# Four-block cross-attention decoder on one core: self attention steps of the last block set among cross steps, queries, keys and values in one arena, the last feed forward in three groups

## The chip, the cores and the metric

The kernel runs on one core of one Trainium2 chip. The metric is the device time of one launch in microseconds (us). All data are float32. In the profile PE is the matmul engine (TensorE), PEld its weight loads, DVE the vector engine, ACT the scalar engine, POOL GpSimd, SP the queue that issues most DMAs. `mm` and `s` are PSUM tiles, all else in these lines is SBUF.

## The reference

Input `x` is 8 batches of 112 rows of 256; the context `ctx_768` is 8 batches of 375 rows of 192. Four blocks follow each other, each adding to `x`:

```
block 0, 1:  x += SelfAttention(norm(x))       16 heads of 64
             x += CrossAttention(norm(x), ctx) 16 heads of 64, 375 keys
             h = norm(x) @ Wp + bp;  a, gate = halves of h (1024 each)
             x += (a * gelu(gate)) @ Wf + bf
block 2:     x += CrossAttention(norm(x), ctx) 16 heads of 64
block 3:     x += SelfAttention(norm(x))       16 heads of 16, causal and key mask
             x += CrossAttention(norm(x), ctx) 16 heads of 16, key mask
             x += gelu(norm(x) @ mlp1 + b1) @ mlp2 + b2        (1024 inner)
```

Attention is softmax(q k^T scaled) v per head, then an output product and its bias. `norm` is a layer norm with gain and bias. The blocks' weights differ.

## The kernel before

**Stages.** The ten lines above are stages 0 to 9: 0 self, 1 cross, 2 feed forward, 3 self, 4 cross, 5 feed forward, 6 cross (block 2), 7 self, 8 cross and 9 feed forward (block 3). `x` lies in seven tiles of 128 rows, the 896 rows of all batches one after another, so a tile spans two batches, and `last_batch(t)` is the last batch that tile `t` needs. `hT` (normed input, transposed) and `oT` (attention output or the feed forward's inner values, transposed, 8 pieces of 128) are one tensor each, for all 896 columns, written and read in parts by all stages.

**Steps.** Attention is cut into steps in the list `steps`: 2 a batch in stages 0 and 3 (8 heads each), 4 a batch in stages 1, 4, 6 and 8 (4 heads each), 1 a batch in stage 7 (16 heads). A step (`add_step`) has three parts on PE: S, the scores into a tile of `ps_s` (L905); T, transposes of the probabilities in banks of four (L924), evicted to `wT`; and PV (L948), evicted to `oT`. Between S and T lies the softmax. In stages 1, 4 and 6 it is a negated maximum on DVE (L872), exponentials on ACT with their sums (L878), a reciprocal on DVE (L884) and a multiplication of each probability tile on POOL (L885). In stages 7 and 8 DVE adds the mask and finds the bound in one instruction a head (L861), ACT takes the exponentials (L865), and the division comes after PV: item R takes reciprocals (L982) and POOL copies them to `rb` (L983); item N transposes `rb` on PE (L989), evicts it as `rT`, and POOL scales `oT` with it (L993).

**Items.** Everything else is an `Item` of a planner (`Plan`), with a cost, a due step (`deadline`), what it uses, what it makes and what it depends on. `add_products` multiplies `oT` by an output weight for one row tile (L587), adds it to `x` (L591), and runs the next stage's norm: statistics on DVE (L525, L527, L529), a power on POOL (L531), the normed tile `xn` on POOL (L533), the bias row added to `x` on POOL (L535). `add_norm_transposes` makes a group of `hT` (L556); the groups are tiles 0-1, 2-3, 4-5 and 6. `add_pair_projection` makes four q or k units for a pair of batches (L620); `add_last_projection` and `add_self_values` do the same for block 3 (L642, L669). Keys and values of the context are jobs in two halves (L710 and L719 for keys, L744 and L753 for values; in stage 8 also L787 to L809), of which up to two are opened at the end of a step and closed at the start of the next one. The function `evac` chooses ACT or DVE for an eviction by a running estimate of their load.

**Order.** PE's instructions run in the order in which the planner emits them; the other engines' are ordered by the framework's scheduler. The list of steps falls into three segments: stages 0 and 1, 3 and 4, 6 to 8. A feed forward's items belong to the next segment. In each iteration the planner emits S of step i+2, PV of step i, T of step i+1, and between the T banks fillers that are ready, earliest due first, as many as `pace` asks for:

```python
for i in range(lo - 2, hi):
    left = plan.pace(i, seg)
    plan.close_jobs()
    plan.main(("S", i + 2)); plan.main(("PV", i))      # where these exist
    for k in range(n):
        plan.main(("T", i + 1, k))
        left -= plan.fill(min(left, share))
    plan.fill(left)
    plan.open_jobs(2, i + 3.5)
```

What is not there when a step needs it is emitted just before it (`require`). Ahead of a segment `drain` emits whatever is ready until the first steps' inputs exist, and after the last step until nothing is left. Items that make q, k or v aren't taken over 8 steps ahead of their due step.

**Buffers.** Weights pass through a ring of 7 buffers, bias rows through one of 2; loads are issued on SP in the order of the `add_*` calls as buffers come free. The ring also holds the mask bytes (`m8`) and two buffers `cm` of masks for four batches each, which come right after `m8` in that order. `add_masks` makes the self mask `cmask` (L495, L496) and eight context masks (L514), all on POOL. q, k and v have rings of 8, 9 and 9 buffers (448, up to 448, and 512 elements a partition). PSUM has four `mm` tiles and two `s` tiles.

**Last feed forward.** `ff_stage` (L1159 matmuls, L1166 GELU on ACT straight from PSUM) takes columns in two groups, `FFG = [(0, 512), (512, 384)]`, after the last step's S; `add_products` then takes the seven row tiles and writes them out.

## Time and profile before

| | us |
|---|---|
| median of 3 runs | 1685.27 (1681.66 to 1685.77) |
| the profiled execution | 1682.51 |
| its span, first to last instruction | 1680.7 |
| granted clock, mean | 0.998 |

| stage | first S at, us | | stage | first S at, us |
|---|---|---|---|---|
| 0 self | 29.5 | | 6 cross | 1094.4 |
| 1 cross | 170.9 | | 7 self | 1398.0 |
| 3 self | 558.6 | | 8 cross | 1460.5 |
| 4 cross | 696.4 | | 8, last S | 1618.9 |

The three feed forwards' matmuls stand at 468.9 to 525, 1005 to 1071 and 1625 to 1667. An engine's busy time is the union of its instructions' times. Matmuls are pipelined and their ends are modelled, so short gaps between them count as busy. In a line of the timeline the columns are the start, the length, the engine, the line of the code, the operation, output<-inputs, shape and count, and in brackets the idle time of the engine before it with what ended it. In a line of waits they are who waited for whom, us in total, times, the longest. In a line of stretches they are the stretch, its length, busy time and count of PE, PEld, DVE, ACT and POOL, the clock granted to PE, the DMAs' share and GB/s.

### The profile page before, as it was taken

To read this page: it belongs to the slowest core of one execution; us is meant where nothing else is said; L and a number is where in the kernel's file an instruction comes from. 1 tells how busy PE (TensorE), PEld (TensorE's weight loads), DVE (VectorE), ACT (ScalarE), POOL (GpSimd) and SP (SyncE) were. 2 spreads that over 40 slices of the span, in tenths; PEclk is the share of its full clock that TensorE was granted. 3 is DMA by queue.
4 is the path that set the end of the run, shared out by engine and by line. 5 is a ranking of instruction groups with operands and counts; after the bars stand their busy time and mean duration, and the time that the engine had idled before them with its cause. 6 is when DMAs were issued, how large, how long until landed. Compare 5 with 4: busy or idle time off the path is not lost.

```text
span 1680.7 us, 30104 instructions
## 1 busy us (share of the span) xinstructions
PE 1644.6 (98%) x11740; PEld 1139.4 (68%) x11740; DVE 847.6 (50%) x2275; ACT 750.0 (45%) x2390; POOL 730.6 (43%) x705
## 2 busy tenths in 40 slices
PE   8999999999999999999999999999999999899999
PEld 7777666666657878676666665766666667666657
DVE  3454454555532344445545552245554558877751
ACT  3454444444431444344444442144443447766661
POOL 1323455556632223355655660474546654332210
PEclk9999999999999999999999999999999999999999
DMA  5011020000101011000000010000000010000000
GB/s 185 4 50 56 3 86 1 1 26 1 51 29 44 1 29 51 26 1 29 2 1 26 1 45 29 11 26 1 1 20 1 1 40 30 2 2 2 2 1 22
DMA packets 26564, 39.48 MB, mean 23 GB/s; under 512 B 1543, under 2 KB 21559, under 8 KB 26423
## 3 DMA queue, kind: packets, MB, share of 16 engines
q1 hardware_dynamic: 25495, 36.74, 6.9%
q8 instruction: 92, 1.51, 0.4%
q10 hardware_dynamic: 864, 0.79, 0.1%
q14 instruction: 49, 0.40, 0.1%
q0 software_dynamic: 64, 0.05, 0.0%
HBM read 35.88 MB, written 0.92 MB: 22 GB/s over the span
## 4 chain that ended last, share of the span: by engine, by line
PE 87%; DVE 5%; issue 3%; ACT 3%; POOL 2%; DMA 0%; POOLq 0%; ACTq 0%; DVEq 0%
PE mm L587 11%; PE mm L620 11%; PE s L905 10%; PE mm L924 10%; PE mm L948 9%; PE mm L710 8%; PE mm L744 7%; PE mm L1159 5%; PE mm L719 4%; PE mm L753 4%; PE mm L669 4%; DVE pr L861 2%; ACT pr L865 2%; PE mm L642 1%; PE mm L556 1%
## 5 line engine op out<-in xcount | busy, mean ns | idle before, releaser
L885 POOL TENSOR_SCALAR pr<-pr,rinv 112x375 f32<-112x375 f32 x384 | 468.8, 1239 | 347.0 <-DVE rinv L884 346.9
L878 ACT ACTIVATE pr<-s,nm 112x375 f32<-112x375 f32 (+1 forms) x640 | 301.8, 489 | 169.6 <-DVE nm L872 169.6
L924 PE MATMUL mm<-ident,pr 112*128 112x112 f32 (+2 forms) x1920 | 233.6, 264 | 10.2 <-ACT oT L307 3.7
L924 PEld LDWEIGHTS mm<-ident,pr 112*128 112x128 f32 (+2 forms) x1920 | 208.6, 151 | 45.9 <-issue 14.0
L872 DVE TENSOR_REDUCE nm<-s 112x2 f32<-112x750 f32 (+1 forms) x224 | 206.4, 958 | 59.3 <-PE s L905 55.3
L307 ACT COPY wT<-mm 128x448 f32<-128x448 f32 (+2 forms) x271 | 141.8, 531 | 180.1 <-PE mm L924 180.0
L948 PEld LDWEIGHTS mm<-wT,v 128*64 128x64 f32 (+5 forms) x3840 | 159.6, 129 | 81.7 <-issue 34.1
L905 PE MATMUL s<-kT,qT 64*112 64x375 f32 (+3 forms) x1792 | 207.2, 392 | 0.0
L948 PE MATMUL mm<-wT,v 128*64 128x112 f32 (+5 forms) x3840 | 200.6, 264 | 3.0 <-ACT wT L307 1.9
L905 PEld LDWEIGHTS s<-kT,qT 64*112 64x112 f32 (+1 forms) x1792 | 112.8, 173 | 73.4 <-issue 22.9
L889 POOL TENSOR_TENSOR pr<-pr,rinv 112x896 f32<-112x896 f32 x32 | 53.9, 1684 | 214.4 <-DVE rinv L888 196.0
L865 ACT ACTIVATE pr<-pr,nm 112x112 f32<-112x112 f32 (+1 forms) x256 | 123.9, 486 | 50.9 <-DVE nm L861 50.8
L315 DVE COPY wT<-mm 128x448 f32<-128x448 f32 (+2 forms) x209 | 125.8, 612 | 16.6 <-PE mm L924 14.1
L878 ACT ACTIVATION_READ_ACCUMULATOR pr<-s,nm 112x1 f32 x640 | 133.1, 208 | 0.0
L315 DVE COPY kT<-mm 128x375 f32<-128x375 f32 (+1 forms) x117 | 65.4, 559 | 131.4 <-PE mm L719 115.5
L315 DVE COPY v<-mm 128x512 f32<-128x512 f32 (+2 forms) x73 | 50.5, 692 | 139.3 <-PE mm L753 119.0
L307 ACT COPY kT<-mm 128x375 f32<-128x375 f32 (+1 forms) x107 | 51.2, 478 | 130.9 <-PE mm L719 118.3
L531 POOL TENSOR_TENSOR rs<-ve,mhalf 128x1 f32<-128x1 f32 x70 | 39.5, 565 | 144.5 <-DVE ve L529 141.9
L591 DVE TENSOR_TENSOR x<-mm,x 128x256 f32<-128x256 f32 x70 | 29.5, 421 | 132.5 <-PE mm L587 132.5
L884 DVE RECIPROCAL rinv<-sums 112x1 f32<-112x1 f32 x384 | 62.6, 163 | 66.8 <-ACT pr L878 57.4
L710 PE MATMUL mm<-ctxA,L_xattn_Wk 128*128 128x375 f32 x256 | 91.5, 480 | 0.4 <-ACT hT L303 0.4
L744 PE MATMUL mm<-L_xattn_Wv,ctxA 128*128 128x512 f32 (+1 forms) x192 | 90.8, 595 | 0.4 <-ACT hT L303 0.4
(140 smaller groups left out, 2364.7 us busy)
## 6 DMA issues: line engine op xcount, KB each, us to landing
L_xattn_Wo<-in_L_xattn_Wo_dram SPq DMA_DIRECT2D x3, 1024.0 KB, 17.8
L_xattn_w_ff<-in_L_xattn_w_ff_dram SPq DMA_DIRECT2D x3, 1024.0 KB, 5.2
L_xattn_Wv<-in_L_xattn_Wv_dram SPq DMA_DIRECT2D x4, 512.0 KB, 6.2
L_xattn_Wq<-in_L_xattn_Wq_dram SPq DMA_DIRECT2D x2, 1024.0 KB, 4.9
L_xattn_Wp<-in_L_xattn_Wp_dram SPq DMA_DIRECT2D x2, 1024.0 KB, 5.3
L_xattn_wq<-in_L_xattn_wq_dram SPq DMA_DIRECT2D x2, 1024.0 KB, 4.7
L_xattn_wo<-in_L_xattn_wo_dram SPq DMA_DIRECT2D x2, 1024.0 KB, 5.3
L_xattn_mlp_w<-in_L_xattn_mlp_w_dram SPq DMA_DIRECT2D x2, 1024.0 KB, 4.9
```

Of the source, the lines that this page charges most:

```text
L307: nc.scalar.copy(dst, src)
L315: nc.vector.tensor_copy(dst, src)
L587: nc.tensor.matmul(ps[:, :D], lhsT=oT[:, c, t * P : (t + 1) * P], rhs=got[wv or w][:, c, :], start=(c == 0), stop=(c == n - 1),)
L620: nc.tensor.matmul(ps[:, i * 2 * T : (i + 1) * 2 * T], lhsT=got[w][:, k, m * P : (m + 1) * P], rhs=hT[:, k, lo:hi], start=(k == 0), stop=( ...
L710: nc.tensor.matmul(ps[:, :S], lhsT=got[wv][:, (2 * u + i) * P : (2 * u + i + 1) * P], rhs=ctxA[:, cols], start=True, stop=False,)
L744: nc.tensor.matmul(ps[: KCH[c][1], :], lhsT=lhs(ctxA, slice(0, KA), c), rhs=got[w][:, hf * 512 : (hf + 1) * 512], start=True, stop=False,)
L872: nc.vector.tensor_reduce(nm[:, :, :ns], sv, AX.X, ALU.max, negate=True)
L878: nc.scalar.activation(pr[:, bk, sl, :], sv[:, bk, sl, :], AF.Exp, bias=nm[:, bk, sl : sl + 1], accum_out=sums[:, bk, sl : sl + 1],)
L885: nc.gpsimd.tensor_scalar_mul(pr[:, bk, sl, :], pr[:, bk, sl, :], rinv[:, bk, sl : sl + 1])
L905: nc.tensor.matmul(tiles[i][:, n % 2, (n // 2) * nk : (n // 2 + 1) * nk], lhsT=qap(h), rhs=kap(h), start=True, stop=True,)
L924: nc.tensor.transpose(pt[:kl, i * T : (i + 1) * T], cell[h][:, c * P : c * P + kl], ident[:T, :T])
L948: nc.tensor.matmul(po[p0 : p0 + dp, blk * T : (blk + 1) * T], lhsT=got[vk][:kl, hv * dp : (hv + 1) * dp], rhs=wt, start=(c == 0 and par(h) ...
```

## The change

It does five things. (1) Steps: the eight self steps of stage 7 no longer stand between stages 6 and 8. Batch 0's stands after the second cross step of batch 4 of stage 6, batches 1 to 3 after the second of batches 5 to 7; batches 4 to 7 after the second step of batches 0 to 3 of stage 8. Due steps are now looked up in `at[(stage, batch, part)]`. (2) q, k and v lie in one tensor of 12224 elements a partition, the size of the three rings together; `find` takes the lowest free place for q and k and the highest for v; a place is free when every item that uses its key has been emitted. (3) The last feed forward takes its first layer in groups of 512, 256 and 128 columns, due within stage 8; the first two groups are evicted with their bias alone, and GELU runs later over `oT` in place, four pieces at a time, after the last exponentials. (4) The `cm` buffers come after the `kv` weights in the order of loads, and the masks' due steps change. (5) The look-ahead is 7 steps, and a job isn't opened ahead of its segment. Dependencies that held block 3's k and v back until stage 6 had made its last are gone. The rest of the code only moves.

```diff
+LASTG = [(0, 512), (512, 256), (768, 128)]
...
+    def find(self, keys):
+        held = sorted(p for k, p in self.place.items() if self.refs.get(k, 0) > 0)
+        out = []
+        for k in keys:
+            n, at = self.size(k), None
+            if k[0] == "v":
+                end = self.arena
+                for lo, hi in reversed(held):
+                    if end - hi >= n:
+                        break
+                    end = lo
+                at = end - n if end >= n else None
+            else:
+                at = 0
+                for lo, hi in held:
+                    if lo - at >= n:
+                        break
+                    at = hi
+                at = at if at + n <= self.arena else None
...
-            if len(self.opened) == n or it.deadline > until:
+            if len(self.opened) == n or it.deadline > until or it.seg > seg:
                 break
...
-            if it.deadline > self.step + 8 and any(k[0] in self.rings for k in it.makes):
+            if it.deadline > self.step + self.ahead and any(k[0] in "qkv" for k in it.makes):
                 continue
...
-    RINGS = {"w": 7, "q": 8, "k": 9, "v": 9, "row": 2}
+    RINGS = {"w": 7, "row": 2}
+    ARENA = 12224
...
+    arena = const.tile([P, ARENA], F32, name="arena")
...
+    def place(key):
+        lo, hi = plan.place[key]
+        t = arena[:, lo:hi]
+        return t if hi - lo != 4 * T else t.rearrange("p (i t) -> p i t", i=2)
...
-        plan.add(Item(("mask", "self"), 0, self_mask, info[7][1] - 14, uses=[src], seg=SEG[6]))
+        plan.add(Item(("mask", "self"), 0, self_mask, first_of(7, 0) - 8, uses=[src], seg=SEG[6]))
+        yield
...
-                plan.add(Item(("mask", b), 0, ctx_mask, info[7][1] + b, uses=[src, key], seg=SEG[7]))
+                plan.add(Item(("mask", b), 0, ctx_mask, first_of(8, b) - 5, uses=[src, key], seg=SEG[7]))
...
-                t = (qpool if ring == "q" else kpool).tile([P, 2, 2 * T], F32, tag=ring, name=ring + "T")
+                t = place(key)
...
-        after = [(("kj", 6, B - 1, 3), 0)] if ring == "k" else []
...
+    per = {0: 2, 1: 4, 3: 2, 4: 4, 6: 4, 7: 1, 8: 4}
+    order = [[(st, b, g) for b in range(B) for g in range(per[st])] for st in (0, 1, 3, 4, 6, 8)]
+    after = {(6, 4): 0, (6, 5): 1, (6, 6): 2, (6, 7): 3, (8, 0): 4, (8, 1): 5, (8, 2): 6, (8, 3): 7}
+    ff_at = {}
+    for i, part in enumerate(order):
+        for st, b, g in part:
+            (self_step if st in (0, 3) else cross_step)(st, 16 if st == 8 else 64, b, g)
+            if g == 1 and (st, b) in after:
+                self_step(7, 16, after[(st, b)], 0)
...
+    def last_ff(st, w1, bias):
+        for f, (lo, n) in enumerate(LASTG):
+            ready = last_of(8, last_batch(tiles_of(lo, lo + n)[-1]))
...
+                    dst = oT[:, m, lo : lo + n]
+                    if f < 2:
+                        evac(dst, ps[:, :n], n, None, col(bias, m))
+                    else:
+                        tc.keep_in_program_order(nc.scalar.activation(dst, ps[:, :n], AF.Gelu, bias=col(bias, m)))
...
+                        ("ff", st, f, m), 8 * n / 2400, fn, ready + (3.5 + 0.7 * m, 2.5 + 0.2 * m, 5 + 0.1 * m)[f],
...
+                def fn(lo=lo, n=n):
+                    for m in (0, 4):
+                        v = oT[:, m : m + 4, lo : lo + n]
+                        tc.keep_in_program_order(nc.scalar.activation(v, v, AF.Gelu))
...
+                        deps=[(("ff", st, f, m), 1.0) for m in range(8)] + [(("S", len(steps) - 1), 4.0)],
...
-    add_masks()
+    masks = add_masks()
+    next(masks)
...
     add_last_ctx(w("kv"), L3 + "k_w", L3 + "v_w")
+    next(masks, None)
     add_row(("row", 8), L3 + "out_b")
...
-            plan.open_jobs(2, i + 3.5)
+            plan.open_jobs(2, i + 3.5, seg)
```

## The prediction

> **What bounds the kernel now.** I read the page first, then the busy time by stretch, the timeline of the places where PE stands still, and the list of waits. The page's engine line and the busy line of the matmul engine in 40 slices:
>
> ```profile
> PE 1644.6 (98%) x11740; PEld 1139.4 (68%) x11740; DVE 847.6 (50%) x2275; ACT 750.0 (45%) x2390; POOL 730.6 (43%) x705
> ...
> PE   8999999999999999999999999999999999899999
> ```
>
> PE is the bound, and the change takes no matmul away. It can win only what PE loses, 1680.7 - 1644.6 = 36.1 us of idle and any half-speed time. So I asked where that lies: busy time of each engine in stage 6 (blocks' third cross attention), stage 7 (the self steps), stage 8 in two parts, and the tail.
>
> ```profile
> 1135.00:1380.00 245.00, 244.56 (x1699) 162.41 (x1699) 131.31 (x304) 105.93 (x297) 135.96 (x117) 1.00 0.03 10
> 1395.00:1460.00 65.00, 57.17 (x747) 45.38 (x745) 57.47 (x343) 51.72 (x263) 19.88 (x34) 1.00 0.06 20
> 1460.00:1560.00 100.00, 95.37 (x999) 62.47 (x998) 75.35 (x253) 66.11 (x198) 28.52 (x48) 1.00 0.01 2
> 1560.00:1623.00 63.00, 57.28 (x680) 37.39 (x676) 49.61 (x176) 45.13 (x137) 14.64 (x22) 1.00 0.01 2
> 1623.00:1680.00 57.00, 53.55 (x248) 37.02 (x248) 7.12 (x18) 14.89 (x26) 3.68 (x6) 1.00 0.05 17
> ```
>
> Columns are length, then PE, PEld, DVE, ACT, POOL busy, granted clock, DMA share, GB/s. Stage 6 loses 0.4 us in 245. Stages 7 and 8 lose 7.8, 4.6 and 5.7 us, with DVE at 88%, 75% and 79%: softmax there is short of matmuls to hide behind. One more loss is at the start of stage 6, first on POOL, then on PE, then in the clock column:
>
> ```profile
> 1116.99 4.84 POOL L514 TENSOR_SCALAR cm<-m 112x375 f32<-112x375 uint8 x4
> 1121.91 0.57 POOL L531 TENSOR_TENSOR rs<-ve,mhalf 128x1 f32<-128x1 f32 x1
> 1122.46 2.47 POOL L885 TENSOR_SCALAR pr<-pr,rinv 112x375 f32<-112x375 f32 x2
> 1124.91 2.46 POOL L533 TENSOR_SCALAR xn<-x,mv,rs 128x256 f32<-128x256 f32 x2
> ```
> ```profile
> 1121.37 0.87 PE L556 MATMUL mm<-ident,xn 128*128 128x128 f32 x6
> 1126.21 0.69 PE L556 MATMUL mm<-ident,xn 128*128 128x128 f32 x2 [3.97 <-POOL xn L533]
> ```
> ```profile
> 1125.00:1130.00 5.00, 3.79 (x16) 3.56 (x17) 1.58 (x3) 1.35 (x3) 5.00 (x6) 0.50 0.17 60
> 1130.00:1135.00 5.00, 5.00 (x18) 3.19 (x16) 0.00 (x0) 1.00 (x2) 1.19 (x1) 0.84 0.07 22
> ```
>
> Four context masks stand on POOL ahead of a norm; PE waits 3.97 us and then runs at half clock. Last, the tail on PE:
>
> ```profile
> 1627.85 1.30 PE L948 MATMUL mm<-wT,v 128*32 128x112 f32 x24
> ...
> 1629.57 12.18 PE L1159 MATMUL mm<-hT,L_xattn_mlp_w 128*128 128x512 f32 x28
> ...
> 1656.69 10.48 PE L1159 MATMUL mm<-hT,L_xattn_mlp_w 128*128 128x384 f32 x32
> 1667.01 10.52 PE L587 MATMUL mm<-L_xattn_mlp_w,oT 128*128 128x256 f32 x48
> ```
>
> After the last PV (L948) PE runs dense: two thirds of the last first-layer matmuls and all its products.
>
> **The change, part by part**, against this execution (span 1680.7, time 1682.5; the median of the runs is 1685.3, 2.8 above it).
>
> *Context masks moved.* Eight L514 of 1.16 us leave the start of stage 6 for its end: their buffers now queue behind `kv`. Without the 4.84 us, L531 starts at 1117.1 and xn is ready near 1122, when PE asks. Saved: the wait, 3.97; the clock, 3.79 x 0.50 + 5.00 x 0.16 = 2.7; together 6.7. L531 and L533 stay, so I take 6.2 (bounds 0, if something else stands in front of xn, and 6.7). The 9.3 us of masks land in POOL's idle 45% of stage 6; should that cover go, each costs at most its 1.16. The self mask (L495, L496) stays where it was, since `drain` still emits it when nothing else is ready.
> The trace has the clock at 0.50 after 3.97 us of idle. [...]
>
> *Self steps among cross steps.* Eight steps of 7.8 us each (their score matmuls start from 1398.0 to 1453.0; stage 8's first at 1460.5). Four go into batches 4 to 7 of stage 6. A step brings ACT 16 exps at a 0.37 us period, 6.0 us, and DVE 16 x 0.19 = 3.1 us, beside evictions. Stage 6 has 9.6 us of PE a step with ACT 43% and DVE 54% busy; four cross steps and one self step come to ACT about 54% and DVE 59%. Cover is ample: these four lose nothing, -3.9 (half of 7.8). The other four stand in batches 0 to 3 of stage 8. Half of stage 8 plus half of stage 7 is DVE 90, ACT 80, PE 107 us: DVE at 85%, hardly better than now, so -1.1. Sum -5.0. Bounds: -12.4 (all of 7.8 + 4.6) and +2 (the mix idles 12% like stage 7 now: 107/0.88 = 121 against 114.5, less the 3.9 and some of the mask term). Data are early enough: each self step comes at least six cross steps after its last input row, 25 us or more, against a chain of product, norm, transpose and projection of some 10 us by the rows (L591 0.42, L525 to L529 0.74, L531 0.57, L533 1.23, L556 0.66, an eviction 0.55, L642 1.6, 0.6 more, and waits).
>
> *First layer of the last feed forward, early and in three groups.* 12.18 + 10.48 - 3.5 (128 of 384 columns remain) = 19.2 us leave the tail. They become fillers of stage 8's last three batches, where PE idles 5.7 us. Only that is won; 13.5 us lengthen those steps. The 16 added bias evictions (0.59 on ACT or 0.69 on DVE for 512 columns) spread over longer steps, DVE falling from 79% to about 70%. Taken -4.2, bounds -5.7 and 0.
> GELU now runs in place at the end, four instructions: L1166 took 0.69 for 512 and 0.58 for 384 columns, 0.86 ns a column, so 2.0 for 2048 and 1.1 for 1024 (estimate). ACT's last exp ended at 1623.2; table 1.28 and 4.0 bring group 0 to 1628.5, PE's last PV to 1629.1. Evictions of the last `wT` may queue behind it: +1.0 (0 to +4). The third group's GELU before the last product: +0.6 (0 to 1).
> In the trace the first GELU starts at 1627.26, right behind the 1.28 us load. [...]
>
> *POOL's queue.* In stage 6 POOL also multiplies every probability tile (L885, 4.96 us a step, ahead of the transposes). Behind it or ahead of it now stand four self steps' `rb` copy, `oT` scale and `v` memset (0.40, 0.66, 0.31). In stages 7 and 8 these wait long at no cost, for nothing else is queued:
>
> ```profile
> POOL oT L993 <- DVE rT L315: 56.7, 11, 18.3
> ...
> POOL v L689 <- PE mm L948: 28.2, 10, 6.6
> ```
>
> POOL has 9.6 x 45% = 4.3 us of slack a step. Taken +1.5; bounds 0 and +28 (12 waits of 6.6, 2.3 over the slack each).
>
> *Arena.* Same 12224 elements a partition as 8 q, 9 k and 9 v buffers. A place is reused only after its readers were emitted on PE, and the matmul that refills it comes later on the same queue, so the eviction's new wait is over already. The page shows no wait of S (L905, 0.0 idle) for q or k. 0; bounds 0 (nothing to gain where PE idles 0.4 in 245) and +8 (one late key or value eviction of 0.5 to 0.7 us plus its wait in each stage-6 batch).
>
> *Planner.* Look-ahead of 7 and jobs kept in their segment: the value and key jobs that ran among feed-forward matmuls at 1008 to 1028 run after them, dense both times: 0 (-1 to +2). Loads on SP stay in one order; row 8 now waits for the second mask buffer, so for the last value job of stage 6, some 25 us before its user needs a 10 us chain: 0 (0 to +5).
>
> *Gaps that count as busy.* Median start-to-start spacing by form leaves 24.5 us more lost from 1400 to 1640 than at stage 6's rate, against 19.2 of shown idle; of the other 5 I take -3 (-5 to 0).
>
> Sum: -6.2 - 5.0 - 4.2 + 1.0 + 0.6 + 1.5 - 3.0 = -15.3: 1667 for this execution, **1670** against the median.
>
> **Rivals.** (1) The waits only move: self steps carry theirs into the mix and the early matmuls lengthen stage 8 in full. For: DVE stays at 85%. Only the masks are won: 1685.3 - 6.2 = 1679 (1674 to 1690 with the small costs). (2) Slower: POOL's in-order queue in stage 6. A scale or memset that waits for PE or an eviction stands ahead of L885, so transposes come late and PE stops. It decides from waits over 4.3 us; priced at its bound +28 less 1.5, 1697 (1690 to 1710). For: waits of 6.6 and 18.3 us exist. Against: they come up where POOL is idle anyway, and the scheduler puts an instruction where it expects it to be ready. (3) Slower: the arena is guarded as a whole, every eviction waiting for all reads before it: 56 jobs in each of three cross stages at 0.5 us, +84. Against: `oT` and `hT` are single tensors written in pieces now, and PE's waits for them are a few us. (4) The early matmuls aren't placed early, for want of weights or buffers: then term three is 0, 1674, inside (1).
>
> **Numbers.** Forecast 0.64, own range 1655 to 1679; (1) with (4) 0.20; (2) 0.12; (3) 0.04. 1654 is all idle and lost clock of these stretches with the hidden 5; 1690 is the top of (1). 1654 to 1690 holds 0.84. This kernel's measurement tells 0.3% (5 us): faster is under 1680, slower over 1690. Faster 0.64 + 0.11 of (1); same 0.08 of (1) + 0.01 of (2); slower the remaining 0.16.
>
> **What would show it.** Right: no L556 wait over 1 us and clock 1.00 in stage 6; PE idle near 0 through the self steps there; L1159 of 512 columns before the last PV and 31 to 33 us from the last PV to the end (49 now); L885 with no late neighbours. Wrong: PE idle in the mixed part of stage 6 behind POOL or DVE; PE idle of stage 8 unchanged with longer steps; a product waiting for GELU; PE waits over 2 us for q, k or v.

## The result: 1.0017 of the time before, and where the expected gain went

| | us |
|---|---|
| before, median of 17 runs | 1683.84 (1681.66 to 1685.77) |
| after, median of 17 runs | 1686.58 (1685.67 to 1688.53) |
| ratio, 95% interval | 1.0017 (1.0010 to 1.0025) |
| the profiled execution after, its span | 1686.16, 1684.4 |

The forecast was 1670 us, faster by 15. The kernel is slower by 2.9 us by the ratio (2.7 by the medians). That is less than the 0.3% that the prediction called measurable, but the interval leaves out 1. In the lines below most line numbers stand 41 above those of the kernel before: the normed tile `xn` (L533) is L574 now, the multiplication of the probabilities (L885) is L926. The page of the kernel after, its engine line for PE and PE's line of the 40 slices:

```profile
PE 1646.4 (98%) x11772; PEld 1145.1 (68%) x11772; DVE 850.0 (50%) x2275; ACT 757.8 (45%) x2402; POOL 728.7 (43%) x705
...
PE   8999999999999999999999999999999998989998
```

PE's busy time is what it was (1644.6 before), and its idle time, 1684.4 - 1646.4 = 38.0 us, is not lower than the 36.1 of before. The change took nothing out of the idle time; it moved the places where PE stands still. The same table as in the prediction, busy time by stretch (columns as there), shows to where: stage 6 before the first self step, the mixed part of stage 6, the mixed part of stage 8, the rest of stage 8, the tail.

```profile
1136.00:1265.00 129.00, 128.56 (x889) 87.16 (x885) 67.88 (x159) 55.81 (x158) 73.29 (x64) 1.00 0.00 1
1265.00:1425.00 160.00, 152.63 (x1221) 103.50 (x1221) 95.70 (x327) 79.71 (x282) 93.48 (x93) 0.99 0.04 12
1425.00:1531.00 106.00, 99.26 (x1101) 70.75 (x1099) 81.51 (x330) 73.87 (x257) 30.64 (x49) 1.00 0.04 13
1531.00:1634.00 103.00, 97.89 (x1004) 62.45 (x1000) 75.71 (x268) 69.48 (x216) 20.30 (x34) 1.00 0.01 2
1634.00:1684.00 50.00, 43.56 (x288) 37.59 (x284) 9.79 (x30) 18.84 (x36) 6.08 (x8) 0.97 0.06 19
```

Plain stage 6 is still dense (0.4 us of idle in 129). But stage 6 with four self steps in it now loses 7.4 us, which is what stage 7 lost alone (7.8), the mixed part of stage 8 loses 6.7, the rest 5.1, and the tail 6.4 where it lost 3.5.

Idle time leaves out half speed and short gaps, so a second ledger was made: the span of a stretch less its matmuls' count by the median start-to-start time of each form. The work that is subtracted is the same in both kernels, 1539.5 and 1539.6 us.

| us lost in | before | after | e17, the best kernel below |
|---|---|---|---|
| 1120 to 1160, start of stage 6 | 8.6 | 6.6 | 2.3 |
| 1160 to 1280 | 7.0 | 7.8 | 7.1 |
| 1280 to 1440, end of stage 6 and on | 15.7 | 20.8 | 18.0 |
| 1440 to 1600 | 27.4 | 23.9 | 23.1 |
| 1600 to the end | 9.6 | 12.0 | 11.8 |

Taken as after less before, the rows are -2.0, +0.8, +5.1, -3.5 and +2.4; with +0.8 ahead of 1120 they add up to +3.6, and the spans differ by 3.7. So two predicted gains are there in part (the start of stage 6, stage 8), and two places are new: the end of stage 6 and the tail. Three readings of the trace after show what stands there.

**Start of stage 6.** The masks are gone from POOL, and PE waits for `xn` (L574) all the same. POOL first, then PE:

```profile
1113.32 0.57 POOL L572 TENSOR_TENSOR rs<-ve,mhalf 128x1 f32<-128x1 f32 x1 [0.47 <-DVE ve L570]
1120.07 2.45 POOL L926 TENSOR_SCALAR pr<-pr,rinv 112x375 f32<-112x375 f32 x2 [6.17 <-DVE rinv L925]
1122.50 2.44 POOL L574 TENSOR_SCALAR xn<-x,mv,rs 128x256 f32<-128x256 f32 x2
```
```profile
1123.79 0.44 PE L597 MATMUL mm<-ident,xn 128*128 128x128 f32 x2 [3.02 <-POOL xn L574]
```

The power L572 is done at 1113.9 for one tile. POOL then stands 6.17 us before two multiplications of probabilities (L926) whose reciprocal DVE has not made, and `xn` is behind them in the queue. The first of two arrives at 1123.7, PE waits 3.02 us (3.97 before), and 3.41 us at half clock, a granted clock of 0.50, follow (6.83 before).

**End of stage 6.** The norms of block 3 are now among the cross steps. POOL, then PE:

```profile
1408.17 4.85 POOL L555 TENSOR_SCALAR cm<-m 112x375 f32<-112x375 uint8 x4
1413.10 0.57 POOL L572 TENSOR_TENSOR rs<-ve,mhalf 128x1 f32<-128x1 f32 x1
...
1415.79 0.56 POOL L572 TENSOR_TENSOR rs<-ve,mhalf 128x1 f32<-128x1 f32 x1
1416.29 0.40 POOL L1024 COPY rb<-rsum 112x256 f32<-112x256 f32 x1
1416.63 0.32 POOL L728 MEMSET arena<- 128x256 f32 x1
1416.93 2.46 POOL L926 TENSOR_SCALAR pr<-pr,rinv 112x375 f32<-112x375 f32 x2
1419.37 1.24 POOL L574 TENSOR_SCALAR xn<-x,mv,rs 128x256 f32<-128x256 f32 x1
```
```profile
1409.36 1.04 PE L628 MATMUL mm<-squares,oT 128*128 128x256 f32 x4
...
1415.82 0.44 PE L597 MATMUL mm<-ident,xn 128*128 128x128 f32 x2
1420.66 1.18 PE L597 MATMUL mm<-ident,xn 128*128 128x128 f32 x6 [4.41 <-POOL xn L574]
```

Four masks (L555), the `rb` copy (L1024), the memset of a `v` (L728) and two probability tiles (L926) share POOL with two norms. The last norm's product ends at 1410.4 (the second L628, start 1409.36) and its `xn` at 1420.6: 10.2 us, where the planner lets the transposes (L597) go 4.5 us after the product (`add_norm_transposes`: `deps=[(("norm", st, t), 4.5) for t in ts]`). PE waits 4.41 us and then has 3.41 us at half clock, which is worth another 1.7; 6.1 us are lost by this alone. In the kernel before the list of PE's waits from 1360 to 1480 has none for `xn`.

**Tail.** ACT, then PE:

```profile
1643.02 1.28 ACT L1260 ACT_TABLE_LOAD   x1
1644.31 3.71 ACT L1260 ACTIVATE oT<-oT 128x2048 f32<-128x2048 f32 x2
1647.93 2.15 ACT L343 ACTIVATE oT<-mm,vcols 128x256 f32<-128x256 f32 x5
```
```profile
1643.03 3.72 PE L1236 MATMUL mm<-hT,L_xattn_mlp_w 128*128 128x256 f32 x16
1648.44 1.78 PE L1236 MATMUL mm<-hT,L_xattn_mlp_w 128*128 128x256 f32 x7 [1.69 <-ACT oT L343]
```

The second group of the first layer (256 columns, L1236) did not get in before the last PV. Its bias evictions (L343) on ACT wait behind the table load and the in-place GELU, five of them until 1647.93; PE then waits 1.69 us for them, while DVE, which could have taken them, stands still for 12.4 us: `evac` weighs the two engines by an estimate that does not know of this GELU. The tail also has 3.41 us at half clock, from 1639.55, but these follow a wait of 1.95 us for `wT` that the kernel before has too (the last section). From the end of the last PV to the end of the span it is 1684.4 - 1643.1 = 41.3 us, where it was 1680.7 - 1629.1 = 51.6 (the prediction wrote 49); the prediction had 31 to 33.

### The profile page after: what moved, and what is told of

The parts are those of the page before. It is cut to its first block, busy times and chain, and to the rows that moved or that the text cites. A ratio compares the mean times of both kernels' runs of the same rounds, so it can differ in the third digit from the quotient of the medians.

```text
span 1684.4 us, 30185 instructions
## 1 busy us (share of the span) xinstructions
PE 1646.4 (98%) x11772; PEld 1145.1 (68%) x11772; DVE 850.0 (50%) x2275; ACT 757.8 (45%) x2402; POOL 728.7 (43%) x705
## 4 chain that ended last, share of the span: by engine, by line
PE 89%; DVE 5%; ACT 4%; POOL 1%; issue 1%; DMA 0%; ACTq 0%; POOLq 0%; DVEq 0%
PE mm L628 12%; PE mm L661 11%; PE s L946 10%; PE mm L965 9%; PE mm L989 9%; PE mm L749 8%; PE mm L783 7%; PE mm L1201 6%; PE mm L758 5%; PE mm L792 4%; PE mm L708 4%; DVE pr L902 2%; ACT pr L906 2%; PE mm L1236 1%; ACT pr L919 1%
## 5 line engine op out<-in xcount | busy, mean ns | idle before, releaser
L926 POOL TENSOR_SCALAR pr<-pr,rinv 112x375 f32<-112x375 f32 x384 | 467.9, 1236 | 348.2 <-DVE rinv L925 347.9
L355 DVE COPY arena<-mm 128x375 f32<-128x375 f32 (+4 forms) x204 | 122.4, 610 | 290.9 <-PE mm L758 132.0
L347 ACT COPY wT<-mm 128x448 f32<-128x448 f32 (+2 forms) x276 | 145.0, 532 | 184.3 <-PE mm L965 184.2
L989 PEld LDWEIGHTS mm<-wT,arena 128*64 128x64 f32 (+5 forms) x3840 | 159.9, 129 | 77.6 <-issue 30.9
L347 ACT COPY arena<-mm 128x375 f32<-128x375 f32 (+4 forms) x164 | 84.7, 516 | 273.2 <-PE mm L758 129.3
L946 PE MATMUL s<-arena 64*112 64x375 f32 (+3 forms) x1792 | 207.5, 393 | 0.0
L989 PE MATMUL mm<-wT,arena 128*64 128x112 f32 (+5 forms) x3840 | 198.2, 264 | 2.2 <-ACT wT L347 2.2
L946 PEld LDWEIGHTS s<-arena 64*112 64x112 f32 (+1 forms) x1792 | 112.8, 173 | 75.3 <-issue 26.6
L906 ACT ACTIVATE pr<-pr,nm 112x375 f32<-112x375 f32 (+1 forms) x256 | 123.9, 485 | 46.0 <-DVE nm L902 45.9
L572 POOL TENSOR_TENSOR rs<-ve,mhalf 128x1 f32<-128x1 f32 x70 | 39.4, 564 | 168.3 <-DVE ve L570 166.1
L353 DVE TENSOR_SCALAR arena<-mm 128x448 f32<-128x448 f32 (+2 forms) x77 | 49.5, 643 | 83.6 <-PE mm L792 51.2
```

What stands on the lines that cost most here:

```text
L347: nc.scalar.copy(dst, src)
L355: nc.vector.tensor_copy(dst, src)
L926: nc.gpsimd.tensor_scalar_mul(pr[:, bk, sl, :], pr[:, bk, sl, :], rinv[:, bk, sl : sl + 1])
L946: nc.tensor.matmul(tiles[i][:, n % 2, (n // 2) * nk : (n // 2 + 1) * nk], lhsT=qap(h), rhs=kap(h), start=True, stop=True,)
L989: nc.tensor.matmul(po[p0 : p0 + dp, blk * T : (blk + 1) * T], lhsT=got[vk][:kl, hv * dp : (hv + 1) * dp], rhs=wt, start=(c == 0 and par(h) ...
```

## The experiments

The first theory from these readings: the steps and layers themselves pay a little, and POOL's queue at the end of stage 6 takes it back, the masks above all. Against it stood the prediction's first rival, that waits only move. All kernels were timed in five rounds against the kernel before on the same chip; the ratios below are to it.

**e1, masks held back until the norms are out.** Each mask's item waits for S of a later cross step.

```diff
-plan.add(Item(("mask", b), 0, ctx_mask, first_of(8, b) - 5, uses=[src, key], seg=SEG[7]))
+plan.add(Item(("mask", b), 0, ctx_mask, first_of(8, b) - 5, uses=[src, key],
+              deps=[(("S", first_of(8, b) - (2 if b == 0 else 3)), 0)], seg=SEG[7]))
```

> The changed kernel with one edit: a context mask may be emitted only after S of three steps before its first use (two for batch 0), so that on POOL the masks of batches 4 to 7 (4.85 us) stand behind two norms of stage 8 instead of ahead of them; PE's order is the same. Theory (the masks met block 3's norms at the end of stage 6 as they met block 2's before): PE's wait of 4.41 us for xn goes and with it 3.41 us at half clock (1.7 us): 6 us less than the changed kernel, about 1680.5. Rival (the wait is that of xn behind two L926 in POOL's order, masks or not): PE still waits 3 to 4 us there, less than 1.5 us gained.

Measured 1692.84 us, 1.0044 (1.0031 to 1.0058): slower. POOL at the same place:

```profile
1414.37 0.56 POOL L572 TENSOR_TENSOR rs<-ve,mhalf 128x1 f32<-128x1 f32 x1 [4.57 <-DVE ve L570]
...
1417.55 0.40 POOL L1024 COPY rb<-rsum 112x256 f32<-112x256 f32 x1
1417.88 0.31 POOL L728 MEMSET arena<- 128x256 f32 x1
1418.18 2.47 POOL L926 TENSOR_SCALAR pr<-pr,rinv 112x375 f32<-112x375 f32 x2
1420.63 1.23 POOL L574 TENSOR_SCALAR xn<-x,mv,rs 128x256 f32<-128x256 f32 x1
```

No mask stands here now, and POOL even idles 4.57 us for `ve`, the statistics that DVE makes. Yet `xn` is done at 1421.9, 9.8 us after its product (10.2 in the kernel after), and PE waits 3.96 us: the rival's account of this wait. The masks meanwhile held up a later norm (PE waits 2.56 us until 1462.1, then 6.83 us at half clock), which is part of why the kernel is slower. So at the end of stage 6 the masks were not the cause, and the theory was too narrow: the norm's chain is long there with no mask in it.

**e2, `xn` on DVE.** Only the engine of one instruction changes; PE's order stays.

```diff
-(nc.vector if st == 0 else nc.gpsimd).tensor_scalar(xn, xt, mv[:, 0:1], rs, ALU.subtract, ALU.mult)
+(nc.vector if st in (0, 6, 8) else nc.gpsimd).tensor_scalar(xn, xt, mv[:, 0:1], rs, ALU.subtract, ALU.mult)
```

> The changed kernel with xn of the norms of stages 6 and 8 made on DVE instead of POOL; PE's order is the same. Theory (PE stands behind POOL's in-order queue at both entries, 3.02 us with L926 ahead and 4.41 us with masks ahead, each followed by 3.41 us at half clock): both waits and both half-clock stretches go, 3.0 + 4.4 + 3.4 = 10.8 us less, about 1676. Rival (the power rs, which stays on POOL, is what comes late behind the masks): the first wait goes (4.7 us), of the second at least 2 us and its half clock remain: 5 to 7 us less.

Measured 1681.42 us, 0.9990 (0.9981 to 0.9999): 4.5 us (0.0027) below the kernel after, the rival's account. PE's waits for `xn` fall from 7.4 to 2.3 us, the loss at 1120 to 1160 from 6.6 to 3.2. It is POOL's order that holds `xn` up at the start of stage 6. At its end a wait of 1.9 us with 3.41 us at half clock remains.

**e3, the feed forward as before** (`ff_stage` in two groups with GELU from PSUM, the due steps of stage 9's norms as before) **and e4, the self steps together as before** (between stages 6 and 8), each the kernel after with one part undone.

```diff
-    last_ff(9, w("m1"), L3 + "mlp1_b")
...
+    ff_stage(9, None, w("m1"), L3 + "mlp1_b", AF.Gelu, f9 - 1)
...
```
```diff
-    order = [[(st, b, g) for b in range(B) for g in range(per[st])] for st in (0, 1, 3, 4, 6, 8)]
-    after = {(6, 4): 0, (6, 5): 1, (6, 6): 2, (6, 7): 3, (8, 0): 4, (8, 1): 5, (8, 2): 6, (8, 3): 7}
+    order = [[(st, b, g) for b in range(B) for g in range(per[st])] for st in (0, 1, 3, 4, 6, 7, 8)]
...
-            if g == 1 and (st, b) in after:
-                self_step(7, 16, after[(st, b)], 0)
```

> The changed kernel with the last feed forward as before: two groups, after the last S, GELU from PSUM. Prices the third part. Prediction's account (won: idle of stage 8, 4.2, less 1.6 at the end): 2 to 4 us more than the changed kernel. Account from the two traces (tail after the last PV 41.3 against 51.6, stage 8's idle no smaller): the 10 us come back in the tail and stage 8 shortens by as much: within 2 us of the changed kernel. Rival (the early matmuls cost more than they hide): over 2 us less.

> The changed kernel with the eight self steps back between stages 6 and 8; all else as changed. Prices the first part. Prediction's account (four steps hidden whole, 5.0 us): 5 us more than the changed kernel. Rival (the waits moved with the steps: the mixed part of stage 6 loses 7.4 us of PE, the mixed part of stage 8 6.7): within 2 us, or faster if block 3's norms no longer meet the masks.

e3: 1688.52 us, 1.0031 (1.0019 to 1.0043); e4: 1689.47 us, 1.0035 (1.0022 to 1.0048). By these the new feed forward is worth some 2.4 us and the interleaving 3.0, though both intervals still overlap that of the kernel after. And neither fits a kernel that is slower in all, and e4's trace shows why its number misleads. POOL, then PE:

```profile
1386.15 9.74 POOL L555 TENSOR_SCALAR cm<-m 112x375 f32<-112x375 uint8 x8 [0.22 <-PE mm L758]
1395.99 4.87 POOL L926 TENSOR_SCALAR pr<-pr,rinv 112x375 f32<-112x375 f32 x4
```
```profile
1397.28 0.31 PE L965 MATMUL mm<-ident,pr 112*128 112x112 f32 x1 [1.59 <-POOL pr L926]
1398.49 0.45 PE L965 MATMUL mm<-ident,pr 112*128 112x112 f32 x1 [0.90 <-POOL pr L926]
1399.70 0.45 PE L965 MATMUL mm<-ident,pr 112*128 112x112 f32 x1 [0.76 <-POOL pr L926]
1400.91 0.45 PE L965 MATMUL mm<-ident,pr 112*128 112x112 f32 x1 [0.76 <-POOL pr L926]
```

With the steps together, all eight masks come in one run of 9.74 us, in front of four probability tiles for which PE's transposes wait: 4.0 us in four pieces, and 6.83 us at half clock behind them, 7.4 us in all. That is POOL's queue, the prediction's second rival, with masks in the place of its scales and memsets, and in a kernel without interleaving.

**e5, the arena alone** (steps, feed forward, masks, look-ahead and dependencies as before) **and e6, the masks' late place alone** (the kernel before with part 4; the edit shown is e6's).

```diff
-        plan.add(Item(("mask", "self"), 0, self_mask, info[7][1] - 14, uses=[src], seg=SEG[6]))
+        plan.add(Item(("mask", "self"), 0, self_mask, info[7][1] - 8, uses=[src], seg=SEG[6]))
+        yield
...
-                plan.add(Item(("mask", b), 0, ctx_mask, info[7][1] + b, uses=[src, key], seg=SEG[7]))
+                plan.add(Item(("mask", b), 0, ctx_mask, info[8][1] + 4 * b - 5, uses=[src, key], seg=SEG[7]))
...
```

> The changed kernel with parts 1, 3 and 4 and the look-ahead undone (self steps together, old last feed forward, masks and their buffers in their old places): what is left is the arena and the jobs kept in their segment. Prediction's account (a place is reused only after its readers on PE's own queue): the kernel before within 2 us. Rival (first fit and the filter spoil the planner's order, or an eviction waits for a reader): 3 to 8 us over the kernel before, seen as waits for arena tiles or a thinner start of stage 6.

> The kernel before with part 4 alone: mask buffers after the kv weights, masks due late. Prediction's account: 6 us less than the kernel before, since only POOL's idle time takes the masks. Theory from the traces (with the old step order the masks meet block 3's norms, and the wait at the start of stage 6 has POOL's L885 ahead of xn as well): the first stall shrinks by 2 us, and 4 to 6 us are lost around 1400: 2 to 4 us more than before.

e5: 1684.36 us, 0.9998 (0.9989 to 1.0006): the arena is free. e6: 1681.54 us, 0.9989 (0.9981 to 0.9998), -1.8 us, which neither account had (-6 and +2 to +4): PE still waits 3.0 us for `xn` at the start of stage 6, since POOL idles 3.59 us for `rinv`, the reciprocal that DVE makes, in front of it there too (L886 and L534 are the L885 and L533 of the kernel before):

```profile
1120.19 2.45 POOL L886 TENSOR_SCALAR pr<-pr,rinv 112x375 f32<-112x375 f32 x2 [3.59 <-DVE rinv L885]
1122.63 2.44 POOL L534 TENSOR_SCALAR xn<-x,mv,rs 128x256 f32<-128x256 f32 x2
```

**e7, the in-place GELU counted in ACT's load, and e8, the context masks on DVE**, each on the kernel after.

```diff
                         tc.keep_in_program_order(nc.scalar.activation(v, v, AF.Gelu))
+                    busy("act", 1.6 + 2 * (0.16 + 0.00084 * 4 * n))
```
```diff
-                    nc.gpsimd.tensor_scalar_mul(got[key][:, n, :], got[src][:, c : c + S], NEG)
+                    nc.vector.tensor_scalar_mul(got[key][:, n, :], got[src][:, c : c + S], NEG)
```

> The changed kernel with one line more: the planner's load estimate of ACT counts the in-place GELU, so seven of the eight 256-column evictions go to DVE, which stands idle there. PE's order is the same. Theory (the evictions stand behind 3.7 us of GELU on ACT, PE waits 1.7 us and then goes at ACT's pace): 1.5 to 3 us less than the changed kernel. Rival (PE's speed there is set by the half clock and the products): within 1 us.

> The changed kernel with the eight context masks multiplied on DVE instead of POOL. Theory (after the run with the masks set apart, where PE waited 3.96 us for xn with no mask ahead of it: the norm chain is slower than the planner's 4.5 us, masks or not): the wait near 1420 stays at 3 to 4 us; within 2 us of the changed kernel. Rival (masks anywhere on POOL are what delays the norms): that wait goes, and 5 to 6 us with it.

e7: 1684.97 us, 1.0007 (0.9999 to 1.0016), 1.6 below the kernel after: seven of the eight evictions of the second group moved to DVE and PE's wait of 1.69 us for L1236 went. e8: 1687.57 us, 1.0024 (1.0014 to 1.0035), no gain; PE waits 7.4 us for `xn` as in the kernel after, 4.0 of it at the end of stage 6. After e1 a second sign that the masks are not what makes the norms late.

**e9, a look-ahead of 8, and e10, the steps together with the look-ahead of 8 and block 3's k and v held back.** Part 1 is worth 3 us by e4, part 3 2.4 by e3, part 4 1.8 by e6, the arena 0, and the sum of all is +2.9. Something common had to cost up to 10 us.

```diff
-        self.now, self.step, self.ahead = 0.0, 0, 7
+        self.now, self.step, self.ahead = 0.0, 0, 8
```
```diff
-        plan.add(Item(keys[0], 1.5, fn, deadline, uses=[w], makes=keys, deps=h_deps(st, lo, hi), seg=SEG[st]))
+        after = [(("kj", 6, B - 1, 3), 0)] if ring == "k" else []
+        plan.add(Item(keys[0], 1.5, fn, deadline, uses=[w], makes=keys, deps=h_deps(st, lo, hi) + after, seg=SEG[st]))
...
-                     deps=h_deps(st, b * T, (b + 1) * T), seg=SEG[st])
+                     deps=h_deps(st, b * T, (b + 1) * T) + ([] if wide else [(("vj", 6, B - 1, 2), 0)]), seg=SEG[st])
```

> The kernel after with a look-ahead of 8 steps instead of 7 and nothing else; the order of PE's fillers changes in all cross stages. Each of the three parts is worth 2 to 3 us by the runs so far, and yet the kernel after is 3 us over the kernel before, so something that they share costs 6 to 10 us. Theory: it is the order of q, k and v items that the shorter look-ahead gives. Then 1680 us (-6), with the losses of 1360 to 1440 back at 2.5 us per 40. Rival: the look-ahead does nothing and the shared cost lies in the norms of block 3: 1685 to 1688.

> The kernel with the self steps together (1689.5 us), with the look-ahead of 8 and the dependencies that hold block 3's k and v back until stage 6 has made its last. What stays of the change is the arena, the late masks and the feed forward in three groups, alone 0, -1.8 and -2.4 us. Theory that the shared cost is the planner's order of q, k and v: 1680 us, and the half clock near 1398 is gone. Rival, late masks and the early first layer disturb each other or the norms whatever the order: 1687 to 1690.

e9: 1694.69 us, 1.0065 (1.0053 to 1.0078), worse than either theory said. e10: 1683.83 us, 1.0008 (0.9999 to 1.0016), 4.5 us (0.0027) better than e4 and short of the 1680 expected; the half clock near 1398 is gone, as expected. Both traces have an accident in the tail that hides what they test. ACT in e9, then PE:

```profile
1644.64 1.28 ACT L1260 ACT_TABLE_LOAD   x1
1645.93 3.71 ACT L1260 ACTIVATE oT<-oT 128x2048 f32<-128x2048 f32 x2
1649.55 0.51 ACT L347 COPY wT<-mm 119x448 f32<-119x448 f32 x1
```
```profile
1650.11 0.60 PE L989 MATMUL mm<-wT,arena 119*32 119x112 f32 x8 [5.09 <-ACT wT L347]
```

The scheduler set the table load and the GELU of 3.71 us ahead of the last eviction of `wT` (L347), so the last PV waits 5.09 us, with 6.83 us at half clock: 8.5 us. In e10 the wait is 5.03 us with the same half clock. The prediction's +1.0 (0 to +4) for evictions queued behind GELU is this; 8.5 is over twice its bound.

**e11, 9 us for a norm.** The planner is told what the trace shows.

```diff
-deps=[(("norm", st, t), 4.5) for t in ts], seg=SEG[st],
+deps=[(("norm", st, t), 9.0 if st in (6, 8) else 4.5) for t in ts], seg=SEG[st],
```

> The kernel after with the planner told that a normed tile of stages 6 and 8 is ready 9.0 us after its product is emitted, not 4.5; from the profile it takes 9.8 us from the product's end to the end of xn where PE stands still. PE is given other matmuls meanwhile. Theory that the wait is a misjudged chain: both waits for xn (3.0 and 4.4 us) and the half clock behind them (3.4 us each, 1.7 lost) go, -8 us with what is lost around them: 1679 us. Rival, that at the end of stage 6 there are no other matmuls and what needs the norm only comes later: one wait moves to S or to q, 1684 to 1687.

Measured 1680.15 us, 0.9983 (0.9975 to 0.9992): 5.7 us (0.0034) below the kernel after. The lists of waits of the kernel after and of e11 (total, times, longest):

```profile
PE mm L597 <- POOL xn L574: 7.4, 2, 4.4
```
```profile
PE mm L597 <- POOL xn L574: 3.0, 1, 3.0
```

The wait of 4.41 us at the end of stage 6 is gone and its half clock too (granted clock 1.00 at 1420 to 1440, 0.91 in the kernel after). The other, of 3.0 us at the start of stage 6, stands as it was: there POOL waits for `rinv`, and a later transpose does not help. So one of the theory's two waits went.

**e12, e2 and e7 together.**

> The kernel after with two edits together: xn of stages 6 and 8 on DVE (-5.2 us alone) and the in-place GELU counted as ACT's load, so that the evictions behind it go to DVE (-1.6 us alone). They act in different places, PE's order is the same: 1680 us (-6.8) if they add, faster than the kernel before by 0.2%; 1682 to 1683 if the gains overlap.

Measured 1678.77 us, 0.9978 (0.9970 to 0.9987): the gains add.

**e13 and e14, the accident removed from e9 and e10.** The GELU is emitted behind the last PV.

```diff
-deps=[(("ff", st, f, m), 1.0) for m in range(8)] + [(("S", len(steps) - 1), 4.0)],
+deps=[(("ff", st, f, m), 1.0) for m in range(8)] + [(("PV", len(steps) - 1), 0)],
```

> The kernel after with a look-ahead of 8 (1694.7 us alone) and with the in-place GELU emitted behind the last PV instead of behind the last S. In the trace of the look-ahead alone the table load and the GELU of 3.71 us stood on ACT ahead of the last eviction of wT, PE waited 5.09 us for it and then ran 6.83 us at half clock, so 8.5 us are lost there. Theory, the look-ahead itself is worth nothing and its 8 us are this accident: 1686 us, the time of the kernel after. Rival, the look-ahead of 8 costs in stage 8 (9 us lost per 40 there against 7.7): 1690.

> The kernel with the self steps together, look-ahead 8 and block 3's k and v held back (1683.8 us), with the GELU emitted behind the last PV. Its trace has the same accident (wait for wT of 5.03 us, half clock for 6.83 us). Theory: this was hiding what the early first layer, the late masks and the arena are worth together, 1676 us (-8); it also says that the order of block 3's norms, q, k and v cost the kernel after the rest. Rival: the GELU now holds up the evictions of the second group instead, 1681 to 1683.

e13: 1689.53 us, 1.0036 (1.0023 to 1.0049), the rival's number: 5 us came back, and the look-ahead of 8 leaves the interleaved kernel 3 us slower (three waits for `xn`, 8.7 us, and half clock three times from 1418 to 1487; the granted clock is 0.91 from 1400 to 1440). So the change's 7 was not the common cost. e14: 1680.19 us, 0.9981 (0.9972 to 0.9990); the 0.0027 that it gained over e10 are a good half of what was expected, because in the tail PE now waits for GELU and for POOL:

```profile
1642.65 1.13 PE L628 MATMUL mm<-squares,oT 128*128 128x256 f32 x4 [1.17 <-POOL oT L1035]
1645.13 7.22 PE L628 MATMUL mm<-L_xattn_mlp_w,oT 128*128 128x256 f32 x25 [1.36 <-ACT oT L1258]
```

From e4 to e14 it is 0.0054, 9 us, and neither has the tail's accident. e14's order keeps the masks away from the probabilities (four of them at 1409.9, where POOL had idled 4.58 us). What remains of the change in e14, the arena, the late masks and the early first layer, should bring 0 + 1.8 + 2.4 = 4.2 us by the runs alone; it brings 3.2.

**e15, the three mends together (e2, e7, e11) on the kernel after, and e16, the allowance of e11 on the kernel before.**

> The kernel after with the three edits that gained alone: the 9.0 us allowance for a norm (-6.4), xn of stages 6 and 8 on DVE (-5.2) and the GELU counted in ACT's load (-1.6). The allowance removed the wait at the end of stage 6 and left that at the start, which xn on DVE removes; some 2 us of the two gains are the same wait. 1675 us. If DVE is the bound of the mixed stage and takes the gain back, 1678.

> The kernel before with the 9.0 us allowance alone, to see whether its 6 us belong to the change. Theory: before the change the drain ahead of stage 7 hides the chain of block 3's norms, and the allowance leaves the wait at the start of stage 6 where it is, as it did in the kernel after: 1683 to 1685 us, no gain. Rival, the planner's 4.5 us were too short in both kernels: 1678 us.

e15: 1678.41 us, 0.9972 (0.9963 to 0.9981), 7.6 us (0.0045) below the kernel after but 3 short of the expectation; with `xn` on DVE most of what the allowance buys is bought already (e12 had 0.9978). The expectation's other account, DVE as the bound, gave 1678 as well; the number does not tell the two apart. e16: 1683.69 us, 1.0000 (0.9991 to 1.0009). In its trace PE's wait for `xn` at the start of stage 6 is longer, 5.3 us for 3.97, but nothing is gained at the end of stage 6, where the kernel before has no wait for `xn` to lose. So the allowance is worth nothing before the change and 5.7 us after it: this cost belongs to the change.

**e17, the steps together with the stalls out (e14 with `xn` of stage 6 on DVE), and e18, the same one instruction in the kernel before.**

```diff
-(nc.vector if st == 0 else nc.gpsimd).tensor_scalar(xn, xt, mv[:, 0:1], rs, ALU.subtract, ALU.mult)
+(nc.vector if st in (0, 6) else nc.gpsimd).tensor_scalar(xn, xt, mv[:, 0:1], rs, ALU.subtract, ALU.mult)
```

> The kernel of e14 (self steps together, look-ahead 8, block 3's k and v held back, GELU behind the last PV; 0.9981 of the kernel before) with xn of stage 6 alone on DVE. Its last large stall is the 3.0 us wait for xn at the start of stage 6 with 3.4 us at half clock behind it, 4.7 us. Theory: they go, 1675 to 1676 us, which is below the best kernel with the self steps among the cross steps (e15, 0.9972), so the interleaving would not be what pays. Rival, xn waits for DVE instead: 1679 to 1680, and the two orders are level.

> The kernel before with xn of stage 6 alone on DVE and nothing else. The prediction gave the masks in front of xn 6.2 us. Theory that POOL's queue is what holds xn up there, whatever stands in it: 1678 us (-6), the wait of 4.0 us and the half clock of 6.8 us gone. Rival, rs on POOL still stands behind the four masks and xn comes as late as before: 1682 to 1684.

e17: 1675.83 us, 0.9956 (0.9942 to 0.9970), the best kernel here. e18: 1680.24 us, 0.9979 (0.9971 to 0.9988). In e18 the four masks still stand on POOL (first line), and PE waits 0.43 us for `xn` instead of 3.97 (the second and third lines are PE's):

```profile
1118.49 4.83 POOL L514 TENSOR_SCALAR cm<-m 112x375 f32<-112x375 uint8 x4
```
```profile
1122.87 0.87 PE L556 MATMUL mm<-ident,xn 128*128 128x128 f32 x6
1124.17 0.44 PE L556 MATMUL mm<-ident,xn 128*128 128x128 f32 x2 [0.43 <-DVE xn L533]
```

So at the start of stage 6 one instruction on another engine is worth 3.5 us to the kernel before, twice what moving the masks is worth (1.8) and short of the 6 expected. And e17 beside e15 bears on the main part: with most stalls out, the kernel with the self steps in one piece stands at 0.9956 and the one with them spread at 0.9972. The intervals overlap and the two differ in look-ahead, in the place of GELU and in the norms of stage 8 as well, so neither order is proven the better one. But no run shows a gain from interleaving that is clear of other stalls: in e4's trace the masks in front of the probabilities lose 7.4 us, more than its 3.0. The 10 us that the parts left unexplained are by this sum 5.7 (the norms' wait, e11) and 3.0 (e4's own stall); the other 1.3 are within the intervals of the runs.

## Why the prediction was wrong, point by point

**Masks, -6.2: mis-sized; -1.8 (e6).** The step that failed is "xn is ready near 1122, when PE asks". The lines shown had L885 between L531 and L533, and the prediction moved it up with the rest without asking when its own input comes. Without the masks POOL reaches that L885 sooner and waits there for `rinv` (3.59 us in e6, 6.17 in the kernel after). The bound of 0, "if something else stands in front of xn", was the mechanism; the value lay nearer to it than to 6.2.

**Self steps, -5.0: failed; nothing is shown (e15 against e17).** The steps in stage 6 were to lose nothing, from ACT at 54% and DVE at 59%. The load came out as forecast (from 1265 to 1425 ACT 79.71 and DVE 95.70 of 160 us, 50% and 60%), and PE lost 7.4 us all the same. The four stretches of 40 us from 1280 to 1440 lose 20.8 us where they lost 15.7, and the next 160 us lose 3.5 less. That is the first rival, the waits move; its 1679 us went wrong by the masks' term and the tail. Averages of load hid the cause that the trace shows: POOL's order in the few steps in which block 3's norms, masks, `rb`, memsets and probabilities meet. The claim that data are early enough priced the norm's chain by its rows, without a queue, and looked at the self step that needs the data. PE stood earlier, at the transposes, which the planner lets go 4.5 us after the product; `xn` took 10.2.

**POOL's queue, +1.5: the mechanism of the second rival, and under-sized.** 6.1 us at the end of stage 6 by the trace, 5.7 by e11, nothing in the kernel before (e16). The prediction had counted `rb`, `oT` and the memset ahead of L885, twelve waits of 6.6; what decided was one `xn` behind L885, with no slack to a step in it.

**First layer early, -4.2: right in kind; -2.4 (e3, with the overlap said above).** L1236 of 512 columns ran before the last PV, of 256 columns after it, so the fourth rival (the early matmuls are not placed early) came true for one group of two. The tail after the last PV fell by 10.3 us, where 31 to 33 instead of 49 made it 16 to 18.

**GELU evictions +1.0 and third group +0.6: right in the kernel after, but the bound of 4 was too low.** The wait is 1.69 us, and e7 got 1.6 back; it was 8.5 us where the scheduler set GELU ahead of the last `wT` (e9). The durations were right: 3.71 us for the two of 2048 columns each (predicted 2.0 apiece) and 2.01 for the two of 1024 (1.1 apiece); the load took 1.28 us. In the trace of the kernel after, the load starts 0.02 us after the eviction before it ends, and the GELU 1.29 us after the load starts.

**Arena 0: right** (e5, 0.9998), and with it the third rival falls. **Planner 0:** the look-ahead of 7 suits the change (8 costs it 3 us, e13). **Hidden gaps, -3: nothing;** the lost time rose by 3.6.

Of the signs that the prediction named for its being wrong, "PE idle in the mixed part of stage 6 behind POOL or DVE" came true. Its sum took each gain at its likely value and had no term for one place in which several moved things meet; that place and the wait in the tail took back 6.1 + 1.69 = 7.8 us by the trace. Measured less forecast is 2.9 + 15.3 = 18.2 us, and the terms make up 4.4 (masks), 5.0 (self steps, at nothing), 1.8 (first layer), 3.0 (hidden gaps) and 4.2 (POOL's queue, 5.7 for 1.5), 18.4 together. That the two agree is partly luck, since the self steps' share is not measured alone and each part is known to about 2 us.

## What to carry to other kernels

When work is moved to where engines idle on average, walk through the queue of each engine at that place, instruction by instruction, and ask of each what it waits for; a small one behind a late one decided here, not the load (`xn` behind two probability tiles without their reciprocal, before which POOL stood still for 6.17 us). A part's worth by undoing it can be another stall that its absence makes (e4): look at the trace of the undone kernel before the number is believed. And a planner's constants hold for the neighbourhood in which they were set: 4.5 us for a norm cost nothing before the change and 5.7 us after it.

## What the runs showed of the hardware that was not expected

Half clock came in whole pieces of 3.413 us. In the traces of the kernels before and after, the clock's records between the first and the last change are whole multiples of it: after, three of 3.413 us at a granted clock of 0.50 and between and behind them 293.55 (86 of it), 215.04 (63) and 40.96 (12) at full clock; before, one of 6.827 (2) at 0.50 and 549.55 (161) at full clock. The record ahead of the first half clock is 1112.74 long (326) in both. So the places where the clock changed lie on a grid in each of the two traces. The same wait in the tail, of 1.95 us for `wT`, in the kernel before and in the kernel after:

```profile
1623.82 1.02 PE L948 MATMUL mm<-wT,v 128*32 128x112 f32 x24 [1.95 <-ACT wT L307]
```
```profile
1638.19 0.82 PE L989 MATMUL mm<-wT,arena 128*32 128x112 f32 x24 [1.95 <-ACT wT L347]
```

In the first it lay across a line of the grid, 1.24 us ahead of it and 0.71 behind, and the clock stayed full (granted clock 1.00 from 1623 to 1630). In the second it lay between two lines, and 3.41 us at a granted clock of 0.50 followed, from 1639.55. Over these two traces, from 40 us to PE's last matmul, the grid has 953 pieces at full clock. The four with most PE idle time (1.95, 2.53, 2.98 and 3.02 us) were each followed by half clock, and none of the others, in which PE stood still for at most 1.69 us (1646.75 to 1648.44 in the kernel after). The four stretches at half clock lasted one piece three times and two pieces once, after the 2.53 us in the kernel before; why that one was longer stays open.

The forecast counted half clock only behind the wait of 3.97 us (2.7 us). In the kernel after, 3.41 us at 0.50, worth 1.7 us, came behind each of three waits, of 3.02, 4.41 and 1.95 us. And waits of this length did not always bring it: in e5's execution, 1679.45 us where its runs go up to 1684.82, the mean granted clock was 1.000, with waits of 3.0 and 1.9 us in it. A gain is therefore read from the medians, and the trace tells where to look.
